# A prologue's order: measuring the third group, the second group's score row and the value weights' sums change places

## The chip, the cores and the metric

The kernel runs on one core of a Trainium2 chip. The metric is the device time of one execution, in microseconds (us); less is better. Engines are named as in the profile: PE (TensorE, matmuls and transposes), DVE (VectorE), ACT (ScalarE), POOL (GpSimd) and SP (SyncE, which here only issues DMAs).

## The reference

Input x is 64 graphs of 256 nodes with 512 features, float32; adj is one 256 x 256 matrix of zeros and ones that all graphs share. Two layers follow each other, each on a normalised and rectified copy of x, with x added to the result:

```python
# layer 0
h = relu(layernorm(x));  H = h @ W                      # 512 -> 256
e = leaky_relu(H @ a[0] + (H @ a[1]).T, 0.2) + NEG * (1 - adj)
x = x + concat([softmax(e) @ H, H])
# layer 1, 8 heads of 64
h = relu(layernorm(x))
q, k, v = (h @ W.T + b for each of q, k, v)
scores = where(adj == 0, -inf, q @ k.T / 8)
x = x + softmax(scores) @ v @ Wo.T + bo
```

## The kernel before, in words

The graphs are worked on two at a time: 32 groups of two. What is done to a group is written as Python generators; each `next` on one issues a few instructions and stops. A hand-written string of letters sets the order in which the generators of neighbouring groups are advanced, and with it the order of every engine's queue. PE's order is fixed outright (`in_order`). On the other engines the framework may move an instruction if it sees it ready sooner, except where the code ties it behind another one: `not_sooner` ties an instruction behind the last one issued so far on its engine, `after` behind a named one. Neither is a wait by a semaphore; both fix only the place in the queue.

The steps that matter here, each with its letter in the prologue:

- `first_norm(g)` (line 550, letter n): for the third group (g = 2) it measures the two graphs (two pieces: bn_stats and bn_aggr for each half, and the factors on POOL), normalises a graph on ACT (`norm`) and transposes it (`turn`) with DVE into the tile xt, of which there is one (bufs=1, line 485), from which SP sends it to DRAM (`passed`) and back in other order (`moved`). The last piece of the second group (g = 1) copies `moved` into hT on ACT.
- `first_layer(1)` (line 696, letter s or 1): the second group's products of features, one per half of a graph (`ph`); after the fourth, `score_rows` (line 621): a small transpose on DVE, a DMA of one line to DRAM and a DMA that spreads it over all partitions (`own`). Then e: four ACT additions, the leaky part on DVE, two ACT exponentials; then two multiplications by the mask on DVE; then four attention products `po`, each with its statistics on DVE; then `norm`, `turn` and the way through DRAM for layer 1's operand, and POOL's sums of operands.
- `project(0)` (line 844, letter u, and `next(products)` in the loop): q, k and v of the first group in seven products each (Strassen's scheme, numbered by `seven`), in the order q1 q2 k1 k2, then q6 q7 q5 q4 q3, then k6 k7 k5 k4 k3, then v1 v2 v6 v7 v5 v4 v3. Of the PSUM banks three are held by name: q's `first` and k's product 7 share held1, as does v's `first` later; q7 and v7 share held0. `take` (line 879) moves a bank out through ACT, and in the first group is tied behind the last ACT instruction (`behind = [scalar.last]`), except for v.
- `judge` (letter c): bounds on the weights that decide whether the kernel's assumptions hold; its third to seventh pieces are squarings of small matrices on PE (`square_q`, `square_k`) with copies or sums on ACT.
- `weight_sums` (line 253): the four sums of a weight matrix that the scheme needs, on DVE for q, k and v, on POOL for the output weights; `first_weight_sums` (line 260): the same for layer 0's weights, on POOL, for use from the third group on.
- `last_bias` (line 272, `next(bias)`): the value bias times the output weights, as `bv_rows` on DVE (four operations), a product `pb` on PE, and an addition to b_out. The first of the four is tied behind the transposes that `turn` issued last:

```python
made = vector.tensor_scalar(rows, of, by, None, op0=ALU.mult)
for other in turn_last:
    after(made, other)
```

`turn_last` is set anew at every `turn` that goes by DVE (line 492). The loop of the prologue advances the products by one per step i, 4 to 20, and between them the pieces that its string names; `next(bias)` is called at the ends of steps 16, 19 and 20. After the loop the steady state begins, with the first group's scores (`sc`).

Of the kernel before, what the change touches and what calls it, by code (L numbers as in the profile page):

```python
# [41 lines left out]
def two_gnn_layers(tc, *args):  # L42

    nc = tc.nc
    with tc.tile_pool(name="verdict", bufs=1) as pool:
        wrong = pool.tile([1, 1], I32, name="wrong")
        bounded(tc, *args, wrong)  # L50
        again = nc.values_load(wrong[0:1, 0:1], min_val=0, max_val=1)
        with tc.If(again > 0):
            tc.strict_bb_all_engine_barrier()
            any_inputs(tc, *args)
# [3 lines left out]
def bounded(  # L58
# [35 lines left out]
    NG = B // GB  # L94
# [28 lines left out]
    def not_sooner(engine, operation, *args, **kwargs):  # L123

        last = engine.last
        after(getattr(engine, operation)(*args, **kwargs), last)
# [25 lines left out]
    def load(g, b):  # L152
        xs[g, b] = big.tile([P, NT, D], F32, tag="x", name=f"x{g}_{b}", bufs=8)
        if g in (2, 3):
            not_sooner(sync, "dma_start", xs[g, b], xg[g, b])
        else:
            sync.dma_start(xs[g, b], xg[g, b])
# [95 lines left out]
    def weight_sums(name, engine=vector):  # L253
        w = w_sb[name]
        not_sooner(engine, "tensor_sub", w[:, :, T3, :], w[:, :, W22, :], w[:, :, W12, :])
        engine.tensor_sub(w[:, :, T1, :], w[:, :, W12, :], w[:, :, W11, :])
        engine.tensor_sub(w[:, :, T2, :], w[:, :, W22, :], w[:, :, T1, :])
        engine.tensor_sub(w[:, :, T4, :], w[:, :, W21, :], w[:, :, T2, :])

    def first_weight_sums():  # L260
        w11, w12, w21, w22 = (
            w0_sb[:, 2 * c : 2 * c + 2, h * FH : (h + 1) * FH] for c in range(2) for h in range(2)
        )
        t2, t3, t4 = (w0_more[:, i] for i in range(3))
        not_sooner(gpsimd, "tensor_sub", t3, w22, w12)
        not_sooner(gpsimd, "tensor_sub", w12, w12, w11)
        not_sooner(gpsimd, "tensor_sub", t2, w22, w12)
        not_sooner(gpsimd, "tensor_sub", t4, w21, t2)
# [864 lines left out]
    def take(*names):  # L1133
        for name in names:
            next(work[name])
# [11 lines left out]
    late_loads()  # L1147
    weight_sums("q")
    take(*"uunuu0011")
    order = "- - nss n nn ns s ss ss s s n - n s - s".split()  # L1150
    for i, parts in enumerate(order, 4):
        next(products)
        if i in (4, 6):
            take(*"cc")
        if i == 4:
            take("c")
        if i == 17:
            weight_sums("o", gpsimd)
        if i == 10:
            first_weight_sums()  # L1160
        if i in (6, 10):
            weight_sums("kv"[i // 10])
        if i == 12 and NG > 3:
            load(3, 0)
            load(3, 1)
        for part in parts:
            if part != "-":
                next(norms if part == "n" else pieces, None)
        if i in (16, 19, 20):
            next(bias)  # L1170
# [5 lines left out]
    for g in range(NG):  # L1176
        products = project(g + 1) if g + 1 < NG else iter(())
        pieces = first_layer(g + 2) if g + 2 < NG else iter(())
        for b, parts in enumerate(steps):
# [10 lines left out]
            i, count = -1, sum(part not in "frv" for part in parts)  # L1190
# [410 lines left out]
```

## Time and profile before

| what | us |
|---|---|
| median of 3 runs | 2406.29 (2406.08 to 2409.01) |
| the profiled execution's own time | 2405.35 |
| its span, first to last instruction | 2403.7 |
| PE busy | 2384.2 (99%) |
| DVE, POOL, ACT busy | 1692.1 (70%), 1421.4 (59%), 1021.8 (43%) |
| PE busy from 0 to 103 us | 90.2 |
| PE busy from 103 to 200 us | 96.4 of 97 |
| PE busy from 200 to 2350 us | 2150 of 2150 |
| PE busy from 2350 us to the end | 47.6 of 53.7 |

A line of a table of waits names the engine and the tile that it was about to write, the engine and tile that released it, and the total, the number and the longest of such waits. A line of a timeline gives start and duration, engine, line of the source, operation, tiles out and in, shapes, the number of instructions merged, and in brackets the idle time before it and who ended it. Where a helper issues the instruction, the line is the helper's (L35, L137), so the tiles tell the places apart.

### The profile page before, as it was taken

Reading aid. Unit: us, or ns where it says so; the run is one execution under the profiler, and the core shown is the slowest. Engines: PE = TensorE matmul, PEld = TensorE weight load, DVE = VectorE, ACT = ScalarE, POOL = GpSimd, SP = SyncE. Lnnn points to the kernel's source line nnn. Section 1 sums busy time; section 2 is a strip of 40 time slices with the busy share of each in tenths; the row PEclk is TensorE's granted clock in tenths of the full one; section 3 lists DMA queues with packets and bytes.
Section 4 is the critical chain, followed back from the end, with each engine's and each line's share of the span. In section 5 each row is a group of like instructions: output and inputs, shape, how many; then the busy total and the mean of one; then the engine's idle time right before and its main releaser. Section 6 shows DMA issues by size and latency. Waiting matters only on the chain.

```text
span 2403.7 us, 43081 instructions
## 1 busy us (share of the span) xinstructions
PE 2384.2 (99%) x15824; PEld 2011.0 (84%) x15824; DVE 1692.1 (70%) x3346; ACT 1021.8 (43%) x2017; POOL 1421.4 (59%) x1290
## 2 busy tenths in 40 slices
PE   9899999999999999999999999999999999999998
PEld 8788888888888888888888888888888888888886
DVE  6687766776766767667767677676677676676665
ACT  4444443444444434434434434344444444343431
POOL 3566656556666556566556565665665566656552
PEclk9999999999999999999999999999999999999999
DMA  5344445544454444455444444444554445454331
GB/s 180 118 128 152 137 146 154 166 146 137 137 162 144 156 142 140 140 157 164 145 136 137 155 154 149 150 137 142 159 159 145 136 137 162 149 157 143 111 106 46
DMA packets 272041, 343.76 MB, mean 143 GB/s; under 512 B 25424, under 2 KB 217168, under 8 KB 271824
## 3 DMA queue, kind: packets, MB, share of 16 engines
q1 hardware_dynamic: 271824, 340.95, 45.8%
q8 instruction: 126, 2.06, 0.4%
q14 instruction: 91, 0.75, 0.1%
HBM read 177.22 MB, written 163.64 MB: 142 GB/s over the span
## 4 chain that ended last, share of the span: by engine, by line
PE 97%; DVE 1%; ACT 1%; DMA 1%; issue 0%; POOL 0%; SPq 0%; ACTq 0%; DVEq 0%
PE py L137 16%; PE pq L137 16%; PE pk L137 16%; PE pv L137 16%; PE sc L137 10%; PE pr L137 9%; PE ph L137 8%; PE po L137 5%; DVE st L35 0%; DMA passed<-xt 0%; ACT hT L35 0%; DVE x L35 0%; DMA moved<-passed 0%; PE total L137 0%; DMA x<-in_x_dram 0%
## 5 line engine op out<-in xcount | busy, mean ns | idle before, releaser
L35 POOL TENSOR_TENSOR p<-p 128x512 f32<-128x512 f32 x248 | 386.5, 1570 | 487.0 <-DVE p L35 468.7
L35 ACT ACTIVATE xn<-x,factor 128x512 f32<-128x512 f32 x256 | 194.8, 807 | 337.0 <-POOL factor L35 329.6
L35 DVE TENSOR_TENSOR p<-p,maskT 128x1024 f32<-128x1024 f32 x254 | 327.7, 1311 | 3.9 <-ACT p L35 3.9
L35 DVE TENSOR_TENSOR x<-py,x 128x256 f32<-128x256 f32 x448 | 185.9, 415 | 189.3 <-PE py L137 183.3
L35 ACT ACTIVATE p<-sc 128x512 f32<-128x512 f32 x512 | 257.7, 624 | 139.4 <-PE sc L137 122.8
L35 POOL TENSOR_TENSOR parts<-parts 128x512 f32<-128x512 f32 x248 | 248.0, 1000 | 80.1 <-DMA parts<-rows 57.6
L137 PE MATMUL py<-wo_sb,oT 128*128 128x256 f32 x1024 | 262.4, 379 | 0.6 <-DVE oT L35 0.6
L137 PE MATMUL sc<-q,k 64*128 64x256 f32 x2048 | 252.1, 390 | 1.6 <-ACT p L35 1.6
L137 PEld LDWEIGHTS sc<-q,k 64*128 64x128 f32 x2048 | 204.5, 186 | 49.7 <-issue 25.9
L137 PE MATMUL pk<-hT,wk_sb 128*128 128x256 f32 x1024 | 245.9, 383 | 0.0
L137 PE MATMUL pq<-hT,wq_sb 128*128 128x256 f32 x1024 | 240.1, 382 | 1.1 <-ACT hT L35 0.7
L137 PE MATMUL pv<-wv_sb,hT 128*128 128x256 f32 x1024 | 236.8, 379 | 0.0
L137 PE MATMUL pr<-p,v 128*32 128x256 f32 x4096 | 234.2, 380 | 0.0
L137 PEld LDWEIGHTS pq<-hT,wq_sb 128*128 128x128 f32 x1024 | 191.7, 190 | 36.7 <-issue 10.3
L35 POOL TENSOR_TENSOR factor<-factor,rexp 128x2 f32<-128x2 f32 (+1 forms) x132 | 116.8, 885 | 172.6 <-DVE factor L35 172.3
L137 PEld LDWEIGHTS pk<-hT,wk_sb 128*128 128x128 f32 x1024 | 190.6, 191 | 33.7 <-issue 9.9
L137 PEld LDWEIGHTS py<-wo_sb,oT 128*128 128x128 f32 x1024 | 194.2, 190 | 28.2 <-DVE oT L35 1.1
L137 PEld LDWEIGHTS pv<-wv_sb,hT 128*128 128x128 f32 x1024 | 194.6, 190 | 26.5
L137 PEld LDWEIGHTS pr<-p,v 128*32 128x32 f32 x4096 | 126.8, 110 | 97.8 <-issue 15.6
L137 PE MATMUL py<-wo_sb,o_sums 128*128 128x256 f32 x768 | 197.6, 380 | 0.5 <-DVE x L35 0.5
L137 PE MATMUL pk<-sums,wk_sb 128*128 128x256 f32 x768 | 181.6, 379 | 0.8 <-ACT kept_k L35 0.8
L137 PE MATMUL pv<-wv_sb,sums 128*128 128x256 f32 x768 | 181.5, 379 | 0.6 <-ACT kept_v L35 0.6
(150 smaller groups left out, 4072.9 us busy)
## 6 DMA issues: line engine op xcount, KB each, us to landing
passed<-xt SPq DMA_DIRECT2D x124, 512.0 KB, 3.1
moved<-passed SPq DMA_DIRECT2D x496, 128.0 KB, 3.5
rows<-p SPq DMA_DIRECT2D x124, 512.0 KB, 3.4
parts<-rows SPq DMA_DIRECT2D x496, 128.0 KB, 3.0
x<-in_x_dram SPq DMA_DIRECT2D x64, 512.0 KB, 4.5
out_dram<-x SPq DMA_DIRECT2D x62, 512.0 KB, 4.0
own<-line SPq DMA_DIRECT2D x31, 256.0 KB, 3.2
wq_sb<-in_L_gnn_Wq_dram SPq DMA_DIRECT2D x2, 512.0 KB, 9.3
```

The source lines that it names most:

```text
L35: instruction = getattr(self.engine, operation)(*args, **kwargs)
L137: in_order(nc.tensor.matmul(*args, **kwargs))
```

## The change

One loop of the prologue changes. Its string now issues, in terms of the steps i:

- step 4 (q6): the second group's last copies into hT and both measuring pieces of the third group (before: steps 6, 7 and 8), behind three of `judge`'s pieces that stay;
- step 5 (q7): k's weight sums (before: 6), the second group's last two first-layer products with the score row (before: 6), and the third group's first normalisation (before: 8); step 6: its first `turn` (before: 9);
- step 7 (q4): `judge`'s second squarings (before: 6), layer 0's weight sums (before: 10) and e (before: 9);
- step 8 (q3): the loads of the fourth group (before: 12);
- step 9 (k6): the masks (before: 10, behind v's weight sums); step 10 (k7) and 11 (k5): the attention products (before: 11 and 12); step 12 (k4): v's weight sums (before: 10) and the second group's second normalisation (before: 13), whose `turn` comes in step 13 (before: 14); its last two pieces come in 17 and 19 (before: 18 and 20);
- step 14 (v1) and 16 (v6): the third group's second normalisation and `turn` (before: 15 and 17).

No instruction is added or left out.

```diff
-    order = "- - nss n nn ns s ss ss s s n - n s - s".split()
+    order = "nnn ssn n s - s ss ss s s n - n s - s -".split()
     for i, parts in enumerate(order, 4):
         next(products)
-        if i in (4, 6):
-            take(*"cc")
         if i == 4:
-            take("c")
+            take(*"ccc")
         if i == 17:
             weight_sums("o", gpsimd)
-        if i == 10:
-            first_weight_sums()
-        if i in (6, 10):
-            weight_sums("kv"[i // 10])
-        if i == 12 and NG > 3:
+        if i in (5, 12):
+            weight_sums("kv"[i // 12])
+        if i == 8 and NG > 3:
             load(3, 0)
             load(3, 1)
+        if i == 7:
+            take(*"cc")
+            first_weight_sums()
         for part in parts:
             if part != "-":
                 next(norms if part == "n" else pieces, None)
```

## The prediction

> **What bounds the kernel now.** I read the page first: PE is busy 2384.2 of 2403.7 us, and the slices show it full almost everywhere, so only PE's idle time and its clock can be won. The table of waits, for PE, then says who ends that idle time (columns: total us, times, longest us).
>
> ```profile
> PE po L137 <- DVE e L35: 5.3, 1, 5.3
> PE sc L137 <- ACT p L35: 1.6, 2, 1.3
> PE ph L137 <- ACT hT L35: 1.3, 1, 1.3
> PE pk L137 <- ACT kept_k L35: 0.8, 1, 0.8
> PE pv L137 <- ACT kept_v L35: 0.6, 1, 0.6
> ```
>
> All but 0.3 us of these lie in the first 103 us, the prologue; from 200 to 2350 us the windows show PE busy throughout. The reader is to see one large wait: the second group's attention product `po` waits 5.3 us for its masked edges `e`. The windows table adds its second price (columns: stretch, us, PE, PEld, DVE, ACT, POOL busy, granted clock, DMA share, GB/s).
>
> ```profile
> 72.00:74.00 2.00, 0.58 (x2) 0.52 (x3) 1.88 (x4) 0.00 (x0) 0.00 (x0) 0.58 0.03 9
> 74.00:76.00 2.00, 2.00 (x6) 1.63 (x5) 0.46 (x2) 0.00 (x0) 0.00 (x0) 0.50 0.00 0
> 76.00:78.00 2.00, 2.00 (x6) 1.55 (x6) 1.73 (x5) 0.00 (x0) 0.00 (x0) 0.50 0.00 0
> 78.00:80.00 2.00, 2.00 (x9) 1.63 (x8) 1.14 (x5) 0.00 (x0) 0.72 (x2) 0.72 0.00 0
> ```
>
> After the wait the clock is halved: (0.84 + 1 + 1 + 0.56) x 2 us = 6.8 us at one half, so 3.4 us of work lost. PE's timeline shows both: eight `po` matmuls take 3.76 us at 73.42, and 1.90 at 79.77.
>
> ```profile
> 54.73 3.75 PE L137 MATMUL ph<-w_sb,hT 128*128 128x258 f32 x16 [1.34 <-ACT hT L35]
> 73.42 3.76 PE L137 MATMUL po<-H,e 128*128 128x257 f32 x8 [5.28 <-DVE e L35]
> 79.77 1.90 PE L137 MATMUL po<-H,e 128*128 128x257 f32 x8
> 83.24 3.62 PE L137 MATMUL pv<-wv_sb,hT 128*128 128x256 f32 x16
> ```
>
> Why `e` is late is read in ACT's and DVE's timelines: the row comes late to ACT, and the mask (72.59) then stands behind the value weights' sums.
>
> ```profile
> 66.00 1.70 ACT L35 ACTIVATE e<-own,H 128x256 f32<-128x256 f32 x4
> 68.91 0.63 ACT L35 ACTIVATE e<-e 128x512 f32<-128x512 f32 x1 [0.51 <-DVE e L35]
> ```
> ```profile
> 68.80 2.67 DVE L35 TENSOR_TENSOR wv_sb<-wv_sb 128x512 f32<-128x512 f32 x3
> 72.59 1.29 DVE L35 TENSOR_TENSOR e<-e,maskT 128x512 f32<-128x512 f32 x2
> 88.33 1.30 DVE L35 STREAM_TRANSPOSE xt<-xn 128x512 f32<-128x512 f32 x2 [0.20 <-DMA passed<-xt]
> 89.56 0.45 DVE L35 TENSOR_SCALAR bv_rows<-wo_sb,bv_col 128x512 f32<-128x512 f32 x1
> 90.04 3.21 DVE L35 SCALAR_TENSOR_TENSOR bv_rows<-wo_sb,bv_col,bv_rows 128x512 f32<-128x512 f32 x3
> 96.14 1.30 DVE L35 STREAM_TRANSPOSE xt<-xn 128x512 f32<-128x512 f32 x2
> ```
>
> [...] after 5.28 us idle the clock was halved for 6.8 us[...]; waits of 1.3 us left it at 1.00. [...] the mask's input was complete at 69.54, yet the mask started at 72.59, behind the sums. [...] a POOL sum beside DVE's masking took 2.25 us (103.84) where it takes 1.26 otherwise. [...]
>
> **The change, part by part.** I set out from 47.98 us, where q's product 7 starts; a product is 8 matmuls, 1.73 us from start to start.
>
> *Row sooner.* The second group's last two first-layer products now follow q's product 7, ahead of product 5 and of the second squarings (0.89 us each). They start at 47.98 + 1.73 = 49.71, if hT is there. Its copies now follow ACT's copy of the squared k (ends 48.77); PE started 0.66 us after the first copy's start before, so 49.35 is enough; the `moved` transfers issued at 41.97 and after take at most 4.5 us. The 1.3 us wait goes, and with the gap around it 1.5 us. The rest of the row's path keeps its lengths. Products end 53.3; H's copy, DVE's small transpose and SP's line follow by 0.9 (58.32 to 59.17 before), so line at 54.15, broadcast issued 1.74 later, 55.9, landing after 3.2: 59.1.
>
> *Edges.* ACT's e now follows the second squarings (PE 56.75 to 58.53; ACT done 2.7 us after PE began, as before, 59.4). So e starts at 59.4 instead of 66.00, and its last exponential ends 3.45 to 3.55 later, at 62.9; the masks follow at once since the value sums come later: done 63.65 instead of 73.9. PE reaches `po` after that. The 5.3 us wait, the 3.4 us of halved clock and the wait for kept_k (0.8) go: with small gaps 9.4 us between k's product 6 and v's product 1.
>
> *A new wait.* k's product 7 takes the held bank of q's `first`, which ACT frees by taking q's product 3. That take is tied behind the last ACT instruction named so far, which is now e's exponential. It ends at 62.9 + 0.84 = 63.7, while PE is ready at 58.53 + 1.73 + 1.73 = 61.98. Wait: 1.8 us. Behind k's product 7 stands all of PE's queue; on ACT kept_k stands behind the take. v's product 1 starts at 83.24 - 1.5 - 9.4 + 1.8 = 74.1.
>
> *Measuring.* Eight statistics operations, 2 x 1.95 us with their factors, move into DVE's idle 10.3 us from 41.4 on (x of the third group, issued 34.24, lands in 6.0). Nothing; without that cover 3.9 us of DVE. Four POOL factors, 1.8 us, stand after POOL's sums and are needed at 53.9. k's sums (2.86) come a place earlier, same cover. The first weights' sums (POOL, 3.8) run near 54 to 58, where POOL stood idle. The fourth group's two loads and the third group's first `passed` stand behind the row on SP; they hold the rings some 4.7 us, as at 66.5, with no wait on them near.
>
> *Value sums later.* DVE now has, from the first `po` on (66.5): four rows' normalising and statistics at 1.62, two pairs of factors, k's two additions (0.65 each), the transposes (1.3), then the sums, of which v's product 6 needs three (2.0). Together 6.5 + 0.5 + 1.3 + 1.3 + 2.0 = 11.6, so 78.1. ACT's kept_v, behind two normalisings that wait for the transposes, is ready at about 78.6. PE would be there at 77.6: 1.0 us, and some 0.3 more at product 5.
>
> *The bias rows.* The diff also moves the third group's second transposes to step 16, before the bias rows, and bv_rows is tied behind the last transposes issued (turn_last). Before, these were the second group's (88.33); now they are the third group's, which need the single xt buffer, hence the landing of the transfer before. Chain: first transposes 74.3 to 75.6; `passed` lands 2.6 later, 78.3; second transposes after the sums, 78.9 to 80.2; `passed` behind four `moved` issues (1.76) at 80.25, landing 3.6 later, 83.9; third transposes to 85.15; bv_rows 0.45 + 3.21, to 88.8; PE's `pb` at 88.97. PE would be there at 77.6 + 1.3 + 4 x 1.73 = 85.8. Wait: 3.2 us. It stands ahead of v's last product on PE's queue, and POOL's output-weight sums wait for the rows too, though they end (91.4) before POOL's next operands.
>
> *After.* Scores start at 88.97 + 0.86 + 1.82 = 91.65, against 97.15: 5.5 us sooner. ACT's hT copies, which made `sc` wait 1.3, are then through (landing 89.3, done 90.5): 1.3 to 1.8 more.
>
> The sum: 1.5 + 9.4 - 1.8 - (1.3 + 3.2 - 0.6 for v's old wait, and rounding 0.3, so 3.6) + 1.6 = 7.1 us. Of the profiled execution, 2405.35 (span 2403.7), 2398.3 remain; its own time is 0.9 under the median of 2406.29, which becomes **2399.2**.
>
> Costs that no row of the page shows: how DVE's unpinned additions fall into order, between 0 (k's addition goes first) and 0.7 us on the chain to `pb`; I take 0. The third group's operands come sooner relative to PE, worth nothing as no wait was there.
>
> **Rivals.**
> *The bias rows don't hold PE* (their chain is 3.2 us shorter than I think): 2396.0. For it: transfers of one kind vary by a us each (2.6 against 3.6), though two of them make only 2. Against: the tie is in the code.
> *[...] the clock halves*: 3.4 more, 2402.6. For it: [...] a slower `passed` adds directly. [...]
> *Slower: the broadcast row lands late.* ACT holds e, q's take and kept_k in one line behind it. If the row comes onto the rings after the third group's `passed` and the fourth group's loads (issued 57.3 on, rings full for 5.2), it lands at 64.5, 5.1 late; PE then waits 6.9 us at k's product 7 and the clock halves, 3.4: 7.1 - 5.1 - 3.4 is 1.4 slower, 2407.7; with the clock halved at the bias wait as well, 2411.1. It loses from 3.7 us of lateness on. Against: the row is issued ahead of both on SP.
> *The row is no sooner* is part of this: at half that lateness nothing is left to be told from 2406.
>
> **Chances.** Forecast 0.58 (2397.5 to 2401.3), no bias wait 0.14, halved clock 0.16, late row 0.12, half of it within 0.2% of before. A measurement of this kernel tells 0.2%, 4.8 us, from no change: faster 0.58 + 0.14 = 0.72, same 0.16 + 0.06 = 0.22, slower 0.06. The range takes in the first three: 2395.8 to 2403.
>
> **What would show it.** `ph` of the second group starting near 49.7; e on ACT near 59.4; `po` without a wait; k's product 7 waiting 1.8 us for ACT q; `pb` waiting 3.2 us for DVE bv_rows; clock 1.00 throughout; `sc` with no 1.3 us wait. The prediction is wrong if the row comes later than 61, if bv_rows precedes the third group's transposes, or if the clock is halved again.

## The result, and the profile after

The changed kernel takes 2403.62 us (median of 20 runs, 2402.27 to 2406.38), the kernel before 2406.47 in the same comparison: a ratio of 0.9988, interval 0.9981 to 0.9995. It is faster by 2.9 us, where 7.1 were forecast; the time lies 0.6 us above the range. The profiled execution took 2403.24 us, its span is 2401.6.

The table of waits for PE, after (engine and tile that waited, who released it; total us, times, longest):

```profile
PE pb L137 <- DVE bv_rows L35: 5.6, 1, 5.6
PE pk L137 <- ACT q L35: 1.5, 1, 1.5
PE pv L137 <- ACT kept_v L35: 0.8, 1, 0.8
PE sc L137 <- ACT p L35: 0.3, 1, 0.3
```

The 5.3 us wait of `po` is gone, and a wait of the same size stands at `pb`. PE's timeline shows where the lead is won and lost:

```profile
50.07 3.65 PE L137 MATMUL ph<-w_sb,hT 128*128 128x258 f32 x16
63.95 1.99 PE L137 MATMUL pk<-hT,wk_sb 128*128 128x256 f32 x8 [1.53 <-ACT q L35]
74.43 3.62 PE L137 MATMUL pv<-wv_sb,hT 128*128 128x256 f32 x16
91.89 2.08 PE L137 MATMUL pb<-bv_rows,square_ones 128*128 128x512 f32 x2 [5.61 <-DVE bv_rows L35]
93.75 2.65 PE L137 MATMUL pv<-wv_sb,sums 128*128 128x256 f32 x8
100.18 3.72 PE L137 MATMUL pq<-hT,wq_sb 128*128 128x256 f32 x16
```

The same places before the change:

```profile
94.47 1.02 PE L137 MATMUL pb<-bv_rows,square_ones 128*128 128x512 f32 x2
97.15 2.42 PE L137 MATMUL sc<-q,k 64*128 64x256 f32 x18
102.90 3.72 PE L137 MATMUL pq<-hT,wq_sb 128*128 128x256 f32 x16
```

v starts at 74.43 instead of 83.24, 8.8 us sooner; q of the second group at 100.18 instead of 102.90, only 2.7 sooner. `pb` and the product behind it take 4.44 us (91.89 to 96.33) where they took 2.68 before (94.47 to 97.15). The windows say why (the columns are those of the windows in the prediction; the granted clock is the number behind the five engines' busy times):

```profile
88.00:90.00 2.00, 0.00 (x0) 0.00 (x0) 1.93 (x4) 0.96 (x2) 0.48 (x1) 0.61 0.48 190
90.00:92.00 2.00, 0.11 (x1) 0.12 (x1) 1.79 (x2) 0.18 (x1) 1.92 (x2) 0.50 0.80 231
92.00:94.00 2.00, 2.00 (x3) 0.97 (x4) 0.00 (x1) 0.00 (x0) 1.92 (x2) 0.50 0.97 207
94.00:96.00 2.00, 2.00 (x7) 1.66 (x7) 0.69 (x1) 0.00 (x0) 0.29 (x1) 0.68 0.70 164
```

The clock is halved from 88.5 to 95.3. Half of that lies inside the wait, so it costs 1.8 us here. Before it cost 2.9: the halving began at 72.3, 1.1 us ahead of the wait's end, and `po` and k's product behind it took 6.35 us (73.42 to 79.77), where the changed kernel takes 3.46 for them (65.78 to 69.24). The 3.4 of the forecast was too much.

That `po` no longer waits is read in ACT's and DVE's timelines: e starts 5.9 us sooner, and the masks follow its exponentials at once. The take of q stands behind e and ends at 63.9; k's product 7, which had waited 1.5 us for it, starts then.

```profile
60.08 1.70 ACT L35 ACTIVATE e<-own,H 128x256 f32<-128x256 f32 x4 [0.34 <-DMA own<-line]
63.07 0.82 ACT L35 ACTIVATE q<-pq,bq_sb 128x256 f32<-128x256 f32 x2
```
```profile
62.42 1.47 DVE L35 TENSOR_TENSOR e<-e,maskT 128x512 f32<-128x512 f32 x2
```

Later lines of DVE's timeline show what `pb` waited for:

```profile
79.74 1.29 DVE L35 STREAM_TRANSPOSE xt<-xn 128x512 f32<-128x512 f32 x2
84.66 0.69 DVE L35 TENSOR_TENSOR v<-pv,kept_v 128x512 f32<-128x512 f32 x1 [3.63 <-PE pv L137]
86.32 0.69 DVE L35 TENSOR_TENSOR v<-pv,kept_v 128x512 f32<-128x512 f32 x1 [0.96 <-PE pv L137]
86.92 1.29 DVE L35 STREAM_TRANSPOSE xt<-xn 128x512 f32<-128x512 f32 x2
88.62 3.21 DVE L35 SCALAR_TENSOR_TENSOR bv_rows<-wo_sb,bv_col,bv_rows 128x512 f32<-128x512 f32 x3
```

The third group's transposes (86.92) stand behind two of v's additions. These wait for v's products 5 and 4 on PE, and DVE stands idle for 3.63 and 0.96 us ahead of them. The transfer that frees xt had landed by 84.5: SP's `moved`, which wait for the same landing, went out then:

```profile
81.06 0.34 SPq L35 DMA_DIRECT2D passed<-xt  x1
84.52 1.73 SPq L35 DMA_DIRECT2D moved<-passed  x4
```

### The profile page after: what moved, and what is told of

It is laid out like the page before. It is cut to its first block, busy times and chain, and to the rows that moved or that the text cites. A ratio compares the mean times of both kernels' runs of the same rounds, so it can differ in the third digit from the quotient of the medians.

```text
span 2401.6 us, 43080 instructions
## 1 busy us (share of the span) xinstructions
PE 2383.5 (99%) x15824; PEld 2011.0 (84%) x15824; DVE 1696.1 (71%) x3346; ACT 1021.7 (43%) x2017; POOL 1423.4 (59%) x1290
## 4 chain that ended last, share of the span: by engine, by line
PE 96%; DMA 1%; DVE 1%; ACT 0%; issue 0%; SPq 0%; POOL 0%; ACTq 0%; DVEq 0%
PE py L137 16%; PE pk L137 16%; PE pq L137 16%; PE pv L137 16%; PE sc L137 10%; PE pr L137 9%; PE ph L137 8%; PE po L137 4%; DMA adj_i<-in_adj_dram 0%; DMA moved<-passed 0%; DMA wv_sb<-in_L_gnn_Wv_dram 0%; DMA passed<-xt 0%; DVE xt L35 0%; DVE x L35 0%; ACT hT L35 0%
## 5 line engine op out<-in xcount | busy, mean ns | idle before, releaser
L137 PE MATMUL pq<-sums,wq_sb 128*128 128x256 f32 x768 | 181.5, 379 | 0.8 <-POOL sums L35 0.8
```

The costliest lines, as they stand in the source:

```text
L137: in_order(nc.tensor.matmul(*args, **kwargs))
```

## The experiments

Each run was timed beside the kernel before, whose median was between 2405.30 and 2405.74 us there, so runs are best compared by their ratios to it. The changed kernel's ratio is 0.9988 (0.9981 to 0.9995). Each profile is of one execution, each median of 6 to 21.

| run | median us | ratio to before, interval |
|---|---|---|
| turn behind the bias rows | 2406.72 | 1.0007 (0.9998 to 1.0015) |
| v's additions behind the bias rows | 2400.52 | 0.9979 (0.9970 to 0.9988) |
| before, with the value sums' place alone | 2405.84 | 0.9999 (0.9991 to 1.0007) |
| turn behind the bias rows, e a step later | 2404.70 | 0.9997 (0.9988 to 1.0005) |
| turn behind the rows, ahead of the additions | 2400.47 | 0.9980 (0.9972 to 0.9988) |
| additions behind, value sums at step 7 | 2401.02 | 0.9982 (0.9975 to 0.9989) |
| the same, e a step later | 2398.90 | 0.9975 (0.9966 to 0.9985) |
| all three | 2397.61 | 0.9968 (0.9956 to 0.9980) |

**V's additions out of the way.** In `projection`, for the first group's v:

```diff
+        def add(*operands):
+            if g == 0 and name == "v":
+                not_sooner(vector, "tensor_add", *operands)
+            else:
+                vector.tensor_add(*operands)
...
-        vector.tensor_add(part(1, 1), first, p7)
+        add(part(1, 1), first, p7)
...
-        vector.tensor_add(part(1, 0), second, p16)
+        add(part(1, 0), second, p16)
```

> The changed kernel with the two additions of v's products 5 and 4 tied behind the bias rows on DVE, and nothing else. Theory (the missing 2.4 us of my chain are these two additions, which stand ahead of the third group's transposes and wait for PE): the transposes start when the transfer before them lands, near 84.5 instead of 86.9, bv_rows ends near 89.4, pb waits 3.3 us[...], so the clock stays whole: 4.1 us less than the changed kernel, about 2399.5 us. Rival (the transfer itself is late and the additions only fill the time): pb still near 91.9, no change, about 2403.6 us.

Measured: 2400.52, which is 5.2 us under the kernel before where the changed kernel is 2.9 under it: some 2.4 us better than the changed kernel, not the 4.1 expected. DVE's timeline of this run:

```profile
81.86 1.29 DVE L35 STREAM_TRANSPOSE xt<-xn 128x512 f32<-128x512 f32 x2
86.65 1.30 DVE L35 STREAM_TRANSPOSE xt<-xn 128x512 f32<-128x512 f32 x2 [3.49 <-DMA passed<-xt]
91.49 1.27 DVE L35 TENSOR_TENSOR v<-pv,kept_v 128x512 f32<-128x512 f32 x2
```

From one pair of transposes to the next it is 4.79 us, where it was 7.18 in the changed kernel: 2.4 us, and now the DMA ends the wait. PE's timeline:

```profile
64.64 2.48 PE L137 MATMUL pk<-hT,wk_sb 128*128 128x256 f32 x8 [2.11 <-ACT q L35]
91.62 1.12 PE L137 MATMUL pb<-bv_rows,square_ones 128*128 128x512 f32 x2 [3.21 <-DVE bv_rows L35]
```

`pb` waits 3.21 us, which is the 3.2 of the forecast, and the clock stays whole there (1.00 in every window from 86 to 94 us); of the waits of 2.0 to 3.2 us that the last section counts, half passed like this. The absolute times of this execution are some 2 us later because k's product 7 waited longer (2.11 us for 1.53, though up to there the two kernels are the same) and the clock was halved after it. The order of two additions is thus the whole of what the forecast missed in the length of the wait at `pb`.

**The tie undone by putting the turn back.**

```diff
-    order = "nnn ssn n s - s ss ss s s n - n s - s -".split()
+    order = "nnn ssn n s - s ss ss s s n - - ns - s -".split()
```

> The changed kernel with the third group's second turn put back from step 16 to step 17, behind the bias rows, so that these are tied behind the second group's transposes again. Theory (the tie to the third group's transposes makes pb wait 5.6 us and halves the clock for 6.8 us): bv_rows starts near 81 instead of 88.1, pb starts without a wait near 86.1, the clock stays whole, q of the second group starts near 93 instead of 100.2: 7.1 us less than the changed kernel, about 2396.5 us. Rival (the way of the second group's data through DRAM and POOL's sums is the bound behind it): PE only waits elsewhere, at sc or at q's products with sums, and the time stays above 2401.

Measured: 2406.72, the rival's number, though what PE came to wait for belongs to the third group and not, as the rival had it, to the second. The wait at `pb` did vanish, and q of the second group started at 91.85, 8.3 us sooner than in the changed kernel. It was all given back within some 45 us (k's product behind the wait at `sc` starts at 136.94, in the changed kernel at 134.44):

```profile
PE sc L137 <- ACT p L35: 5.0, 1, 5.0
PE ph L137 <- POOL sums_xn L35: 2.8, 1, 2.8
```

The third group's transposes came no sooner: in DVE's timeline they stand at 86.98 (86.92 in the changed kernel), now behind v's additions and b_out's.

```profile
86.38 0.69 DVE L35 TENSOR_TENSOR b_out<-pb,b_out 128x512 f32<-128x512 f32 x1 [0.17 <-PE pb L137]
86.98 1.29 DVE L35 STREAM_TRANSPOSE xt<-xn 128x512 f32<-128x512 f32 x2
```

PE, 8.3 us ahead, now comes too early for the third group. In ACT's timeline the copy of the third group's second hT stands behind q's last take, which waits for PE:

```profile
104.24 0.84 ACT L35 ACTIVATE q<-pq,bq_sb 128x256 f32<-128x256 f32 x2 [3.32 <-PE pq L137]
104.97 1.13 ACT L35 COPY hT<-moved 128x512 f32<-128x512 f32 x2
```

POOL's sums follow at 106.18, and `ph` waits for them. The wait at `sc` is for exponentials tied behind e of the third group, whose row goes out late: SP issues it behind transfers of the row sums.

```profile
120.36 1.74 SPq L35 DMA_DIRECT2D parts<-rows  x4
122.14 0.54 SPq L35 DMA_DIRECT2D line<-rows  x1
125.00 0.35 SPq L35 DMA_DIRECT2D own<-line  x1
```

The clock was halved at both waits, for 3.4 and 6.8 us (0.72 from 108 to 110, 0.50 from 110 to 112 us; 0.67 from 128 to 132, 0.50 from 132 to 136). So my theory was right on `pb` and wrong on the time: the bias wait hid the next bound. That the transposes are this bound is only argued here; the next run tries it.

**The turn sooner as well.** Both edits together, which give DVE the order: second group's transposes, bias rows, third group's transposes, v's additions.

> The turn behind the bias rows as in the run before, and v's two additions tied behind that turn, so that DVE's order is: second group's transposes, bias rows, third group's transposes, v's additions. Theory (without the bias wait the third group's way is the bound: its transposes stood at 87 us in both kernels, so PE, 8.3 us sooner at q's product 1, waits at ph and at sc): the transposes come at 83.9 instead of 87.0, its operands and its row some 3 us sooner; the wait at ph falls from 2.8 to about 1, that at sc from 5.0 to about 2 to 3, and the time from 2406.7 to about 2402. Rival (the waits at ph and sc come from POOL's queue or from the order of SP, not from the transposes): both waits stay, 2406.

Measured: 2400.47, some 6 us under the turn alone, where 4.7 were expected. The transposes come at 85.15, as the line of DVE's timeline shows; both copies of hT now stand ahead of q's take; the wait at `ph` is gone, and of the waits at `sc` this is left:

```profile
85.15 1.30 DVE L35 STREAM_TRANSPOSE xt<-xn 128x512 f32<-128x512 f32 x2
```
```profile
PE sc L137 <- ACT p L35: 2.8, 2, 2.3
```

The third group's turn was what came next behind the bias rows. What is left at `sc` goes with SP's order as above (the row at 117.38, behind `parts` at 115.60); that this order causes it wasn't tried.

**One part of the change alone.** The kernel before, with the value sums behind the masks:

```diff
-        if i in (6, 10):
-            weight_sums("kv"[i // 10])
+        if i in (6, 12):
+            weight_sums("kv"[i // 12])
```

> The kernel before with one part of the change alone: the value weights' sums at step 12 instead of 10, behind the masks. Theory (that part takes 3.3 us from the wait of po and keeps the clock whole there, but moves 2.8 us of DVE work ahead of the last two rows' statistics and lets v's additions in among the bias rows): po waits about 2 us at 68, v starts near 77, pb then waits about 4 us: about 2403 us, so this part alone does what the whole change does. Rival (the masks were late only because the row was late, and the sums' place is worth nothing): po waits 5 us as before, 2406 us.

Measured: 2405.84, no change. That is the rival's number, but not for its reason: `po` waits 2.0 us and not 5. The waits came as in the theory, and the time didn't:

```profile
PE pb L137 <- DVE bv_rows L35: 3.8, 1, 3.8
PE po L137 <- DVE e L35: 2.0, 1, 2.0
```

v starts 6.1 us sooner than before, counted from q's product 6. At the second group's q 0.8 is left: 3.8 went into the wait at `pb`, and the halved clock took 1.8 on `pb` and the product behind it (2.08 and 2.66 us). I had not counted that. The sums' place is worth its 3.3 us at `po`, and the same 2.8 us of DVE work then lies on the way to the bias rows, among whose four operations two of v's additions stand besides (at 89.19 and 90.45). The other two parts of the change, the row and the measuring, weren't tried alone.

**E behind q's take.** The turn put back, and e at step 8 instead of 7:

```diff
-    order = "nnn ssn n s - s ss ss s s n - - ns - s -".split()
+    order = "nnn ssn n - s s ss ss s s n - - ns - s -".split()
```

> The kernel with the turn behind the bias rows, and e moved from step 7 to step 8, behind q's product 3 and its take. Theory (k's product 7 waits 1.5 us because the take stands behind e's exponentials on ACT): no wait at k's product 7; e starts about 1.3 us later, near 61.4, so that po waits about 0.6 us for the masks; 1.0 us less than with e in step 7, about 2395.5 us. Rival (the time that PE gains there is lost again at v's product 6 or at pb, whose chain hangs on the second group's statistics): no difference to e in step 7.

Measured: 2404.70. k's product 7 no longer waits, `po` waits 0.5, v starts 0.8 us sooner, as expected. The total misses as the run with e at step 7 did, for its reason (`sc` 5.2, `ph` 2.9 us of wait). Between the two, 2.0 us were measured, with intervals that overlap.

**The value sums first.** V's additions behind the bias rows, and

```diff
-        if i in (5, 12):
-            weight_sums("kv"[i // 12])
+        if i in (5, 7):
+            weight_sums("kv"[i // 7])
```

> The changed kernel with v's additions tied behind the bias rows (2400.5 us), and the value weights' sums moved from step 12 to step 7, ahead of e and the masks, where DVE stood idle for 3 us. Theory (with the row sooner, the masks no longer have to pass the sums, and the sums only lengthen the chain to the bias rows at 75 to 79 us): po still without a wait, the second group's second transposes 0.8 us sooner, bv_rows and pb 0.8 us sooner: about 2399.7 us. Rival (the sums delay e's leaky part and the masks by up to 2.7 us as before): po waits and the time rises to 2402 or more.

Measured: 2401.02; against 2400.52 without it neither a gain nor a loss can be told. The sums ran from 58.17 to 61.02 on DVE, e's leaky part followed at 61.39, and `po` didn't wait. So with the row sooner the masks need not pass the sums. But `pb` waited 3.6 us in the profile, and the clock was halved there (its two matmuls took 2.07 us, with the clock whole 1.02); the gain of 0.8 didn't come out. Of it 0.54 us is there at the second group's transposes (4.52 us after v's start, in the run without it 5.06), and 0.45 is lost again before the third group's (5.24 us later for 4.79), which the DMA holds.

**The value sums first, and e behind q's take.** The run before, with e at step 8.

> The same with e moved from step 7 to step 8, behind the take of q's product 3. Theory (everything up to pb hangs on one chain from e over po and the second group's statistics, so that what k's product 7 no longer waits comes through to pb): no wait at k's product 7, po waits about 0.5 us, pb still waits about 3 us, about 0.8 us less than without it: 2398.9 us. Rival (the chain to pb starts from e, which is later now): no gain, or 1 us more.

Measured: 2398.90, the number expected, and in part by luck: `pb` waited 4.1 us and not 3, and the clock was halved there (0.50 from 88 to 92 us). k's product 7 doesn't wait, v starts 1.2 us sooner than in the run before, and `pb` 0.7 sooner after q's product 6 (43.86 us after it instead of 44.53): what is won upstream comes through, since `pb` hangs on the same chain. The 0.7 agrees with the 0.8 expected. The medians lie 2.1 apart, with intervals that overlap, and part of that is the clock: three of the ten executions, the profiled one among them, took 2400.6 to 2400.7 us at a mean clock of 0.998, the other seven 2398.5 to 2399.1 at 0.999.

**All three remedies.**

> The third group's turn behind the bias rows and ahead of v's additions, the value weights' sums at step 7, and e at step 8: all three remedies together. Theory (what comes sooner up to the bias rows now also brings the third group's turn sooner, since the turn hangs on the same chain): the transposes of the third group come 1.5 us sooner than with the turn alone (85.2), pb doesn't wait, sc still waits about 2 us for ACT behind e of the third group: about 2399 us. Rival (the third group's row, which the order of SP's transfers holds, sets the end whatever comes before): 2400.5 us, as with the turn alone.

Measured: 2397.61, the lowest median of all, though of six executions and with an interval that overlaps those of the three runs that come next: 7.7 us under the kernel before (0.9968, where the changed kernel has 0.9988, so some 4.8 us under that). The third group's transposes start at 83.54, `pb` doesn't wait. The largest wait left in PE's table is the one at `sc`, and in this execution the clock stayed whole after it (1.00 from 122 to 128 us):

```profile
PE sc L137 <- ACT p L35: 2.9, 2, 2.3
```

## Why the prediction was wrong

By its steps, forecast and measured:

- *Row sooner*: `ph` at 49.7; 50.07. Right; 0.35 of the difference was there at q's product 6 already (44.72 for 44.37).
- *Edges*: e at 59.4; 60.08, after 0.34 us of wait for the broadcast, which took 3.9 us to land instead of 3.2. `po` without a wait: right.
- *A new wait* at k's product 7: 1.8; 1.53. Right, with its cause, as the runs with e at step 8 show, where it is gone.
- *Measuring* costs nothing: DVE did it from 41.65 in its idle time. POOL's sums kept 1.26 to 1.28 us each. Right for PE; on DVE the work between stretched (k's sums took 3.72 us for 2.86), which still fell into idle time.
- *Value sums later*: 1.0 us at v's product 6; 0.77. V started at 74.43 for 74.1.
- *The bias rows*: the wait at `pb`, forecast at 3.2, was 5.6. The chain was right to within 0.9 us link by link up to the landing of `passed` (83.9; 84.5). Then the third group's transposes started at 86.92 instead of 83.9. **This is the step that failed**: "how DVE's unpinned additions fall into order, between 0 and 0.7 us on the chain to `pb`; I take 0". I bounded an addition by its own 0.65 us. It is worth what it waits for: v's product 4 ended at 86.3, DVE stood idle for 0.96 us until then, and the transposes, whose xt was free at 84.5, stood behind its addition. Measured: 2.4 us, shown by tying the two additions behind.
- *The clock*: forecast whole; halved for 6.8 us, of which 1.8 us of PE's time. **This step failed too**, apart from the additions: a wait of 3.2 us was held safe, which no trace had shown. In this execution the halving began at 88.46, after 2.18 us of idleness; the forecast's own wait, from 86.28 to about 89.5, would have been as long idle by then. That the clock would have been halved in it too is my estimate from these times; no run shows it. With the additions out of the way but the third group's turn still ahead of the bias rows, `pb` waited 3.2, 3.6 and 4.1 us in three profiles, and the clock was halved at the last two. The second rival had this halving, but with 3.4 us as its price. Here it was 1.8, because the halving began inside the wait: 3.4 of the 6.8 us lay ahead of `pb`. Yet that rival kept the rest of the forecast's chain, so the range ended at 2403.0, and the halving and the additions together passed it.
- *After*: the wait at `sc` is 0.3; right.

The sum corrected: 7.1 - 2.9 for `pb` (91.89 for 88.97, of which 2.4 are the additions and the rest is lateness of the chain before them) - 1.8 for the clock + 0.3 for scores a little quicker than forecast is 2.7; the traces show 2.72 at the second group's q, the medians 2.85.

One thing the forecast didn't see was no fault in its number, but in what I took for the gain still to be had: with the bias wait gone because the tie was undone the time is not 2396.0, as the first rival said, but 2406.7, since the third group's turn comes next.

## What to carry to other kernels

When an order written by hand is changed, look through every tie "behind the last one issued": it moves with the order, and here it put the bias rows behind another group's transfer. An instruction that a scheduler may set ahead of the critical one in an engine's queue can cost more than its duration: here, on DVE, the critical one stood behind it until its operand was ready (0.69 us of duration and 2.4 us of delay). And a lead on the busiest engine is kept only if the next group's chain comes sooner by as much: undoing the tie alone lost all that the change had won, and with the next group's turn brought forward too it was worth keeping.

## What the runs showed of the hardware

The forecast held a wait of 3.2 us safe for the clock. The trace before showed 5.28 us with a halving and waits of 1.3 us without one, and nothing between. Where the windows cover a halving from end to end, it lasted 3.4 or 6.8 us. But waits shorter than 3.2 us brought one on: after the 2.11 us at k's product 7 in the run with v's additions behind the bias rows, its windows show

```profile
64.00:66.00 2.00, 1.36 (x6) 1.24 (x7) 0.58 (x1) 1.31 (x4) 0.00 (x0) 1.00 0.05 18
66.00:68.00 2.00, 2.00 (x6) 1.58 (x6) 0.00 (x0) 0.84 (x2) 0.00 (x0) 0.50 0.00 0
```

and it followed 2.85 us at `ph` with the turn put back, and 2.25 us at `sc` with the turn sooner, while 3.21 us at `pb` and 2.33 us at `sc` (all three) passed without it. The length of the wait alone doesn't decide: with the turn sooner the same product 7 waited as long, and the clock stayed whole, as the 2.00 us of its eight matmuls show (2.48 in the run above).

```profile
64.43 2.00 PE L137 MATMUL pk<-hT,wk_sb 128*128 128x256 f32 x8 [2.10 <-ACT q L35]
```

Where the halving began, counted from the start of the wait, is read from the windows:

| run and wait | clock | halving began after the wait's start by, us | lasted, us |
|---|---|---|---|
| before, `po`, 5.28 us | halved | 4.2, inside the wait | 6.8 |
| changed kernel, `pb`, 5.61 us | halved | 2.2, inside the wait | 6.8 |
| sums first and e later, `pb`, 4.12 us | halved | 2.5, inside the wait | 6.8 |
| turn put back, `ph`, 2.85 us | halved | 2.9, at its end | 3.4 |
| additions behind, k's product 7, 2.11 us | halved | 3.5, behind it | not read to its end |
| turn sooner, `sc`, 2.25 us | halved | 2.7, behind it | 3.4 |
| turn sooner, k's product 7, 2.10 us | whole | | |
| additions behind, `pb`, 3.21 us | whole | | |
| all three, `sc`, 2.33 us | whole | | |

From 20 to 240 us the ten traces hold fifteen waits of PE of 2.0 us or more. All seven of 3.6 us or more (3.62 to 5.61) had a halved clock inside or behind them. Of the eight others four had it (2.11, 2.25 and twice 2.85) and four had not (2.02, 2.10, 2.33 and 3.21); the six waits of 1.2 to 1.6 us had none. So the length doesn't separate the eight, and what does is not shown: no run was made to test it. The forecast's 3.2 us lies among them; as an estimate from these eight, such a wait could go either way, and it was not to be held safe. One halving came without a long wait: with the value sums alone the clock was 0.93 from 14 to 16 us and 0.50 from 16 to 18, and the one wait that PE's timeline marks from 12 to 16 us is of 0.40 us (14.21). PE was then at transposes and at products two columns wide; why the clock was halved there, no run here shows.
